# A two-layer attention kernel: the bias table made before the first projection, products of ones in two pauses of the array, and layer 1's weights prepared in the first image

## The chip, the cores and the metric

The kernel runs on one core of a Trainium2 chip. A core has a matrix engine (TensorE, PE in the profile), a vector engine (VectorE, DVE), an engine for activation functions (ScalarE, ACT), a general engine (GpSimd, POOL) and a sequencer that mostly issues transfers (SyncE, SP). Each runs its own list of instructions in order and waits for the others by semaphores. Sixteen DMA engines move data between the memory (DRAM) and the on-chip buffers; SP and ACT put transfers on queues for them. The metric is the device time of one execution in microseconds (us), lower is better.

## The reference, cut to what matters

Eight images of 384 channels and 32 x 32 = 1024 positions pass through two layers in float32. Layer 0 normalizes by groups and applies attention with a position bias, the output of a small network on the relative offset of two positions:

```python
def relative_bias(h, w, w1, b1, w2, b2):
    rel = (coords[:, None, :] - coords[None, :, :]) / denom      # 2 numbers per pair
    hidden = gelu(rel @ w1 + b1)                                 # 192 wide
    return transpose(hidden @ w2 + b2, (2, 0, 1))                # 8 heads

# layer 0 (8 heads of 48)
q, k, v = split(group_norm(x) @ qkv_w + qkv_b)
attn = softmax(q @ k.T * 48**-0.5 + relative_bias(...))
x = x + (attn @ v) @ proj_w + proj_b

# layer 1 (6 heads of 64), on tokens t
q, k, v = split(layer_norm(t) @ qkv_w.T)
q, k = normalize(q), normalize(k)        # each row: less its mean, over its deviation
t = t + (softmax(q @ k.T * 64**-0.5) @ v) @ proj_w.T + proj_b
t = t + bitlinear(gelu(bitlinear(layer_norm(t))))
```

The bias depends only on the offset, so 63 x 63 values per head hold all of it. Layer 1's projection comes after a layer normalization and, for q and k, before a normalization of each head's row. Both means can be taken out of the weights ahead of time: each column of the transposed weight less its mean over the 384 input channels, and each head's 64 columns of q and k less their mean.

## The kernel before, in words

**Layer 0's work.** `_layer0` (line 184) runs the eight images one after another. For each image, `project_qk` (456) makes q and k: three pairs of heads, each with a `pq` tile of 128x1024 for q and one for k, twelve matmul records per tile. Tiles for q are evicted from PSUM by DVE, those for k by ACT. `project_v` (490) makes four `pv` tiles, evicted by DVE. Then 32 units follow: a unit is a pair of heads, a half of the queries and a quarter of the keys. `scores` (514) writes two `s` tiles in PSUM, DVE adds the bias (`e<-s,grow`, line 532), ACT takes the exponential (536), and two units later `weigh` (542) multiplies by v into `o`. All the PSUM tiles come from one pool of four (`mm2`, 111): a fifth tile waits until the first is evicted.

**The bias.** `hidden` (342) runs the network's first layer on the offsets (`rel`, `w1`): 32 matmul records into eight `ph` tiles, and eight Gelu activations on ACT. `table_part` (366) multiplies by `w2` into `pb`, DVE adds `b2`, and SP stores the part to `table` in DRAM, half of the table per call. The attention needs the bias spread out, as `grow` in the on-chip buffer, in 32 parts (8 heads, 4 blocks of rows). `grow_load` (384) fetches a part from `table` with four DMAs of 114.2 KB (`wide<-table`), and `grow_turn` (396) copies it, reversed, into `grow`: even blocks on ACT (401), odd ones on DVE (403). Twenty parts go through a pool of nine `e` tiles, twelve through rows of `oT`, which is where attention outputs go later.

**The order of work.** The engines' lists are in the order in which the Python code calls them. `_Later` (64) delays work: `after(n, work)` has `work` called at the n-th following `step()`. There is a step after each of the six `pq` tiles, each of the four `pv` tiles and each unit. Before the change the start is: group norm's statistics, the weights placed (`place_weights_qk`, 289), both calls of `hidden`, the loads of `bqk`, the normalization applied on DVE, the loads of `wv`, `bv`, `wp`, `wl`, `bp` (`load_weights_v_out`, 318), the first `table_part`, and the second one a step later. Loads of parts begin at step 2, turns one step after their loads.

**Transfers.** All these loads but those of the bias network are issued by SP, in order. Each DMA of SP and ACT reports on one of eight semaphores, taken in turn in program order, and an issue waits until the former transfer on its semaphore has landed.

**Layer 1's weights.** `_Start` (121) loads layer 1's weight (1.77 MB) during the last image of layer 0, at its unit 5, and layer 1's first image at unit 6. Then `means` makes the column sums by products with a tile of ones (`cm`, line 146: twelve records of 128x512 and six of 128x128), ACT scales them (151), POOL subtracts them (158); `heads` sums each head's columns on DVE (164) and subtracts on POOL (166). These steps are called at units 10 to 23.

Of the kernel before, what the change touches and what calls it, by code (L numbers as in the profile page):

```python
# [63 lines left out]
class _Later:  # L64


    def __init__(self):
        self.due = []
# [52 lines left out]
class _Start:  # L121
# [4 lines left out]
    def __init__(self, tc, ins, x1, shared):  # L126
        self.nc, self.ins, self.x1, self.shared = tc.nc, ins, x1, shared

    def load_weights(self):
        self.wqkv = self.shared.weights("wqkv").rearrange("p (k c) -> p k c", k=KC)  # L130
        self.nc.sync.dma_start(
            self.wqkv, self.ins["L1_attn_qkv_wT"].rearrange("(k p) c -> p k c", p=P)
        )
# [5 lines left out]
    def means(self, temp, at, n):  # L139
        nc = self.nc  # L140
        pm = self.shared.mm2(f"cm{at}")
        for h in range(-(-n // HALF)):
            w = min(HALF, n - h * HALF)
            for k in range(KC):
                cols = slice(at + h * HALF, at + h * HALF + w)
                nc.tensor.matmul(
                    pm[:, h, :w], self.shared.ones, self.wqkv[:, k, cols],
                    start=(k == 0), stop=(k == KC - 1),
                )
        self.mean = temp(f"cmean{at}")  # L150
        nc.scalar.activation(
            self.mean[:, :n], pm.rearrange("p h q -> p (h q)")[:, :n], AF.Copy, scale=1.0 / C
        )

    def subtract(self, at, n):
        for k in range(KC):
            w = self.wqkv[:, k, at : at + n]
            self.nc.gpsimd.tensor_sub(w, w, self.mean[:, :n])

    def heads(self, k):  # L160
        nc = self.nc
        w = self.wqkv[:, k, 0 : 2 * C].rearrange("p (h d) -> p h d", d=D1)
        hm = self.shared.pool.tile([P, 2 * H1], F32, tag="hm", name=f"hm{k}")
        nc.vector.tensor_reduce(hm, w, AX.X, ALU.add)
        nc.gpsimd.tensor_scalar(hm, hm, 1.0 / D1, 1.0, ALU.mult, ALU.mult)
        nc.gpsimd.tensor_sub(w, w, hm.unsqueeze(2).to_broadcast([P, 2 * H1, D1]))

    def stages(self, temp):

        first, rest = (0, 2 * HALF), (2 * HALF, 3 * C - 2 * HALF)  # L170
        return [
            (5, self.load_weights),
            (6, self.load_image),
            (10, lambda: self.means(temp, *first)),
            (11, lambda: self.subtract(*first)),
            (12, lambda: self.means(temp, *rest)),
            (14, lambda: self.subtract(*rest)),
            (19, lambda: self.heads(0)),
            (21, lambda: self.heads(1)),
            (23, lambda: self.heads(2)),  # L180
        ]


def _layer0(tc, ins, x1, sums, shared, beside):
# [9 lines left out]
    with ExitStack() as ctx:  # L194
# [31 lines left out]
        QT, QN = 32, 2 * HALF  # L226
# [5 lines left out]
        nc.vector.memset(rel, 0.0)  # L232
        nc.vector.memset(w2, 0.0)
        nc.vector.memset(b2, 0.0)
        for g in range(P // QT):
            at = g * QN
            n = min(QN, NREL - at)
            nc.scalar.dma_start(rel[g * QT : g * QT + 2, 0:n], ins["rel"][:, at : at + n])
            nc.scalar.dma_start(w1[g * QT : g * QT + 2], ins["L0_conv_mlp_w1"])
        with nc.allow_non_contiguous_dma(reason="a bias, once"):  # L240
            nc.scalar.dma_start(b1, ins["L0_conv_mlp_b1"].rearrange("(k p) -> p k", p=HC))
            nc.scalar.dma_start(
                w2[:, :, 0:H0], ins["L0_conv_mlp_w2"].rearrange("(k p) h -> p k h", p=HC)
            )
        for g in range(P // QT):
            nc.scalar.dma_start(b2[g * QT : g * QT + H0], ins["L0_conv_mlp_b2"].unsqueeze(1))
# [9 lines left out]

# [31 lines left out]

        def place_weights_qk():
            whole = 2 * NF0 * D0  # L290
            for s in range(2):
                nc.vector.tensor_copy(
                    wqk[:, :, s, :, 0:D0],
                    raw[:, :, s, 0:whole].rearrange("p k (h d) -> p k h d", d=D0),
                )
                for j in range(2):
                    at = whole + j * D0
                    nc.vector.tensor_copy(
                        wqk[:, :, s, j::2, D0:S0],
                        raw[:, :, s, at : at + D0].rearrange("p k (c d) -> p k c d", d=FR),  # L300
                    )

        def load_bias_qk():
            with nc.allow_non_contiguous_dma(reason="a bias, once"):
                for j in range(2):
                    for row, n, at, step in (
                        (j * S0, D0, j * D0, 2 * D0),
                        (j * S0 + D0, FR, (2 * NF0 + j) * D0, FR),
                    ):
                        for s in range(2):  # L310
                            nc.sync.dma_start(
                                bqk[row : row + n, s],
                                bass.AP(
                                    qkv_b.tensor, qkv_b.offset + s * C + at, [[1, n], [step, NF0]]
                                ),
                            )

        def load_weights_v_out():
            nc.sync.dma_start(wv, qkv_w[:, 2 * C : 3 * C].rearrange("(k p) c -> p k c", p=P))
            nc.sync.dma_start(bv, qkv_b[2 * C : 3 * C].partition_broadcast(P))  # L320
            pw = ins["L0_conv_proj_w"]
            for j in range(2):
                last = (2 * NF0 + j) * D0
                for row, n, at, step in (
                    (j * S0 + SP, D0, j * D0, 2 * D0),
                    (j * S0, FR, last, FR),
                ):
                    nc.sync.dma_start(
                        wp[row : row + n],
                        bass.AP(  # L330
                            pw.tensor, pw.offset + at * C, [[C, n], [step * C, NF0], [1, C]]
                        ),
                    )
                nc.sync.dma_start(wl[j * S0 + SP : (j + 1) * S0], pw[last : last + D0])
            with nc.allow_non_contiguous_dma(reason="a bias, once"):
                nc.sync.dma_start(bp, ins["L0_conv_proj_b"].rearrange("(k p) -> p k", p=P))
# [3 lines left out]
        WR = GW // 4  # L340

        def hidden(r):

            hids = {}
            for k in range(2):
                for a in range(2):
                    ph = mm2(f"ph{r}{k}{a}")
                    for i in range(2):
                        g = 2 * a + i
                        nc.tensor.matmul(  # L350
                            ph[0:HC, i], w1[g * QT : g * QT + 2, ts(k, HC)],
                            rel[g * QT : g * QT + 2, ts(r, HALF)], start=True, stop=True,
                        )
# [12 lines left out]
        def table_part(r, hids):  # L366
            pb = mm2(f"pb{r}")
            for k in range(2):
# [6 lines left out]
            nc.vector.tensor_scalar_add(backwards(part[:, HALF - 1 : HALF], HALF), pb[:, 0], b2)  # L375
            for g in range(P // QT):
                at = g * QN + r * HALF
                n = min(HALF, NREL - at)
# [264 lines left out]
        place_weights_qk()  # L643
        hids = [hidden(r) for r in range(2)]
        stages[3]()
        load_bias_qk()
        stages[4](nc.vector)
        load_weights_v_out()
        table_part(0, hids[0])
        later.after(1, lambda: table_part(1, hids[1]))  # L650
        nc.scalar.activation(tiny[:, 1:2], tiny[:, 0:1], AF.Exp)
# [14 lines left out]
        for i, n in enumerate((3, 3, 3, 3, 2, 2, 2, 2)):  # L666
            later.after(i + 3 + (i > 3), lambda n=n: grow_turns(n))
            later.after(i + 2, lambda n=n: grow_loads(n))
        for i in range(len(parts) - 20):
            later.after(i + 11, lambda: grow_turns(1))  # L670
            later.after(i + 8, lambda i=i: grow_loads(1, 1 + i % NF0))
        qk = project_qk(0, first)
        project_v(0, first)
        with_last = beside(etile)
        for b in range(B):
            held = []
            for i, u in enumerate(units):
# [10 lines left out]
                if b == B - 1:  # L688
                    for at, work in with_last:
# [1130 lines left out]
def tile_conv_attn_hybrid(ctx: ExitStack, tc: tile.TileContext, ins, out):  # L1820
    dram = ctx.enter_context(tc.tile_pool(name="x1", bufs=1, space=DRAM))
    x1 = dram.tile([B, C, N], F32, tag="x1", name="x1")
    state = ctx.enter_context(tc.tile_pool(name="state", bufs=1))
    flag = state.tile([P, 1], mybir.dt.int32, tag="flag", name="flag")
    sums = state.tile([P, B, NP0, 2 * N // P], F32, tag="sums", name="sums")
    with ExitStack() as main, tc.manual_schedule():
        shared = _Shared(tc, main)
        start = _Start(tc, ins, x1, shared)
        before = _layer0(tc, ins, x1, sums, shared, start.stages)
# [6 lines left out]
    with tc.If(out_of_range > 0):  # L1836
        _layer0_shifted(tc, ins, x1)
        with ExitStack() as again, tc.manual_schedule():
            shared = _Shared(tc, again)
            start = _Start(tc, ins, x1, shared)  # L1840
            late = again.enter_context(tc.tile_pool(name="late", bufs=2))
            for _, stage in start.stages(
                lambda name: late.tile([P, N], F32, tag="t", name=name)
            ):
                stage()
# [45 lines left out]
```

## Time and profile before

| what | value |
|---|---|
| median of 3 runs | 3036.66 us (3036.26 to 3038.47) |
| profiled execution's own time | 3039.49 us |
| its span, first to last instruction | 3037.7 us, mean granted clock 0.998 |
| PE busy | 3017.8 us, 99% of the span |
| DVE, ACT, POOL busy | 1775.4, 1401.8, 464.2 us |
| chain that ended last | PE 93%, DMA 3%, DVE 2%, ACT 1% |
| first hidden matmul | 7.41 us |
| first `pq` matmul / first `s` matmul | 23.14 / 73.87 us |

The table comes from the page of the profile and its timeline. All times inside the execution count from the span's start. "Busy" is the time in which an engine carries out instructions, without issuing transfers or waiting. The timeline puts neighbouring instructions of one kind on one row: start, duration, engine, line, operation, tile written and tiles read, and their number; in brackets how long the engine was idle before and what ended it. "PE" are matmuls, "PEld" the loads of their weights, "SPq" and "ACTq" the issue of transfers. One 128x512 float32 product is two matmul records. The granted clock is the share of TensorE's full clock, 1.00 or half of it.

### The profile page before, as it was taken

The page shows a single profiled execution, that of the slowest core. Times are in us where ns is not written, and L with a number is a line of the kernel's source. Part 1 is how long each engine was busy: PE and PEld are TensorE (multiplying, and loading weights), DVE is VectorE, ACT ScalarE, POOL GpSimd, SP SyncE. Part 2 cuts the span into 40 slices and gives each one's busy share as a digit, 9 for nine tenths or more (in the row PEclk, how much of TensorE's full clock was granted, in tenths as well). Part 3 has the DMA queues.
Part 4 walks back from the last instruction along what each step waited for, and adds up shares of the span by engine and source line. Part 5 has one row for each costly group of instructions (what it writes and reads, how often), then busy time and mean ns, then how long its engine had stood idle before and what let it go on. Part 6 is the DMA issues. An engine that isn't in the chain of part 4 may idle for free.

```text
span 3037.7 us, 45667 instructions
## 1 busy us (share of the span) xinstructions
PE 3017.8 (99%) x18914; PEld 1616.1 (53%) x18914; DVE 1775.4 (58%) x1763; ACT 1401.8 (46%) x1759; POOL 464.2 (15%) x315
## 2 busy tenths in 40 slices
PE   9999999999999999999999999999999999999999
PEld 3455546455554645444545655655655655645453
DVE  3746647373654727355564765765765755754646
ACT  2633526253442616244373563553553553553534
POOL 0111102121110202123202202202202202211110
PEclk9999999999999999999999999999999999999999
DMA  7412021211202020121311101101101101102011
GB/s 175 122 26 83 19 82 23 65 37 23 78 21 81 23 78 23 29 96 51 99 43 31 56 16 37 50 16 37 50 23 30 50 23 30 50 16 72 16 51 38
DMA packets 102137, 149.94 MB, mean 49 GB/s; under 512 B 59616, under 2 KB 63184, under 8 KB 101152
## 3 DMA queue, kind: packets, MB, share of 16 engines
q1 hardware_dynamic: 99056, 146.86, 17.2%
q8 instruction: 152, 2.49, 0.3%
q14 instruction: 65, 0.53, 0.1%
q10 hardware_dynamic: 2864, 0.05, 0.1%
HBM read 110.52 MB, written 27.30 MB: 45 GB/s over the span
## 4 chain that ended last, share of the span: by engine, by line
PE 93%; DMA 3%; DVE 2%; ACT 1%; POOL 0%; issue 0%; SPq 0%; DVEq 0%; ACTq 0%; POOLq 0%
PE s L521 15%; PE o L552 15%; PE s L1322 11%; PE o L1371 11%; PE pq L467 8%; PE y2p L1614 6%; PE pq L1178 5%; PE pp L616 4%; PE pv L1259 4%; PE y1p L1563 4%; PE pp L1468 4%; PE pv L495 4%; PE sum L1398 1%; DMA wide<-table 1%; PE hs L1207 1%; DVE lun L1515 1%
## 5 line engine op out<-in xcount | busy, mean ns | idle before, releaser
L536 ACT ACTIVATE e<-e 128x1024 f32<-128x1024 f32 x512 | 535.0, 1057 | 441.7 <-DVE e L532 421.7
L532 DVE TENSOR_TENSOR e<-s,grow 128x1024 f32<-128x1024 f32 x512 | 601.0, 1217 | 190.6 <-PE s L521 190.1
L521 PE MATMUL s<-qk 48*64 48x512 f32 x4096 | 608.0, 592 | 2.6 <-DVE e L532 2.2
L552 PE MATMUL o<-e,v 64*64 64x512 f32 x4096 | 603.5, 591 | 0.0
L1333 ACT ACTIVATE e<-s,kc 128x512 f32<-128x512 f32 x768 | 463.3, 693 | 171.7 <-PE s L1322 161.0
L1322 PE MATMUL s<-qk,qk 64*64 64x512 f32 x3072 | 418.5, 592 | 0.3
L1371 PE MATMUL o<-e,v 64*64 64x512 f32 x3072 | 414.9, 590 | 0.0
L521 PEld LDWEIGHTS s<-qk 48*64 48x64 f32 x4096 | 238.8, 133 | 227.5 <-issue 82.9
L552 PEld LDWEIGHTS o<-e,v 64*64 64x64 f32 x4096 | 259.8, 133 | 178.6 <-issue 76.8
L1348 DVE TENSOR_TENSOR t<-t,e 128x1024 f32<-128x1024 f32 x192 | 230.8, 1221 | 54.0 <-ACT e L1333 53.9
L1322 PEld LDWEIGHTS s<-qk,qk 64*64 64x64 f32 x3072 | 153.8, 132 | 190.0 <-issue 108.8
L1178 PE MATMUL pq<-bx,wqkv 128*128 128x512 f32 x576 | 254.1, 596 | 0.7 <-ACT tra L1150 0.7
L467 PE MATMUL pq<-xn,w 128*128 128x512 f32 x576 | 251.7, 598 | 0.0
L1371 PEld LDWEIGHTS o<-e,v 64*64 64x64 f32 x3072 | 158.2, 133 | 170.5 <-issue 142.9
L581 POOL TENSOR_TENSOR inv<-sums,over 128x16 f32<-128x16 f32 x32 | 92.7, 2898 | 1011.0 <-DMA sums<-sd 852.6
L467 PEld LDWEIGHTS pq<-xn,w 128*128 128x128 f32 x576 | 109.6, 191 | 142.9 <-issue 140.4
L1178 PEld LDWEIGHTS pq<-bx,wqkv 128*128 128x128 f32 x576 | 107.9, 190 | 143.4 <-issue 139.7
L1345 DVE TENSOR_TENSOR t<-e,e 128x1024 f32<-128x1024 f32 x96 | 114.1, 1223 | 81.2 <-ACT e L1333 81.0
L1550 DVE TENSOR_REDUCE parts<-y 128x1 f32<-128x1024 f32 x75 | 90.0, 1217 | 93.1 <-ACT y L1547 92.5
L1228 POOL TENSOR_TENSOR hc<-hc,rsqrt 128x32 f32<-128x32 f32 x24 | 139.4, 5810 | 2.0
L1194 ACT ACTIVATE qsq<-pq 128x1024 f32<-128x1024 f32 x48 | 49.1, 1024 | 190.3 <-DVE qk L1188 102.0
L477 DVE TENSOR_SCALAR qk<-pq,bqk 128x1024 f32<-128x1024 f32 x24 | 30.8, 1284 | 176.9 <-PE pq L467 176.9
(165 smaller groups left out, 3033.9 us busy)
## 6 DMA issues: line engine op xcount, KB each, us to landing
rb<-rd SPq DMA_DIRECT2D x110, 256.0 KB
xn<-in_x_dram SPq DMA_DIRECT2D x24, 512.0 KB
res<-in_x_dram SPq DMA_DIRECT2D x24, 512.0 KB
x<-res SPq DMA_DIRECT2D x24, 512.0 KB
bx<-x SPq DMA_DIRECT2D x8, 1536.0 KB
rq<-hi SPq DMA_DIRECT2D x48, 256.0 KB
out_dram<-bx SPq DMA_DIRECT2D x23, 512.0 KB
wide<-table SPq DMA_DIRECT2D x80, 114.2 KB
```

The source lines that it names most:

```text
L467: nc.tensor.matmul(pq[:, h], wqk[:, k, s, 2 * pair : 2 * pair + 2, :].rearrange("p h d -> p (h d)"), xn[:, k, ts(h, HALF)], start=(k == 0) ...
L521: nc.tensor.matmul(s[j][ts(c, QP), i], qk[pair][rows, 1, ts(4 * m2 + 2 * i + c, QP)], qk[pair][rows, 0, ts(h, HALF)], start=True, stop=True,)
L532: nc.vector.tensor_add(e.rearrange("p (i q) -> p i q", i=2), s[j], bass.AP(near.tensor, near.offset, [near.ap[0], [-QROWS * IW, 2], [1, HA ...
L536: nc.scalar.activation(e, e, AF.Exp)
L552: nc.tensor.matmul(po[ts(j, S0), r], v[keys, 2 * m2 + i, 2 * pair + j, :], es[j][keys, ts(i, HALF)], start=(m2 == 0 and i == 0), stop=(m2 ...
L1178: nc.tensor.matmul(pq[:, h], wqkv[:, k, s * C + pair * P : s * C + (pair + 1) * P], xt[:, k, ts(h, HALF)], start=(k == 0), stop=(k == KC - 1),
L1228: nc.gpsimd.tensor_tensor(c, c, rsqrt.to_broadcast(list(c.shape)), ALU.pow)
L1322: nc.tensor.matmul(s[j][ts(c, QP), i], qk[pair, 1][rows, ts(4 * m2 + 2 * i + c, QP)], qk[pair, 0][rows, ts(h, HALF)], start=True, stop=True,)
L1333: nc.scalar.activation(e[:, ts(i, HALF)], s[j][:, i], AF.Exp, scale=kc[:, pair, j, m : m + 1])
L1348: nc.vector.tensor_add(total[j], total[j], e)
L1371: nc.tensor.matmul(po[ts(j, D1), r], v[keys, 2 * m2 + i, at : at + D1], es[j][keys, ts(i, HALF)], start=(m2 == 0 and i == 0), stop=(m2 == ...
L1614: nc.tensor.matmul(py[m][:, h], w2[:, k, ts(m, P)], supply.parts[k][i][:, ts(h, HALF)], start=(k == 0 and i == 0), stop=(k == FC - 1 and i ...
```

## The change

- **Operands of the network.** `rel` is cut evenly and loaded with two DMAs instead of four, `w1` likewise; only one column is cleared. ACT calls a Gelu on a small tile early and loads `w2` and `b2` after it.
- **Products of ones.** `stir` multiplies the tile of ones by itself, n times, into a PSUM tile that the next real product overwrites: seven before the first hidden product, four before the first table half.
- **Table.** Both halves are made before the first projection, the first evicted by DVE and the second by ACT.
- **Loads moved.** `bqk`, `wv`, `bv`, `wp`, `wl` and `bp` are issued by ACT instead of SP.
- **Layer 1's weights.** `_Weights` loads them in the first image by ACT, ahead of `wv`, into rows of `grow` that are filled last. Column sums are now made by two additions of the three row blocks on POOL and three products; DVE scales, POOL subtracts, `heads` as before; SP stores the result to `ready` in DRAM. In the last image of layer 0 only a load of `ready` and the load of the image are left.
- **Spreading the table.** The first three parts are loaded before `project_qk`, the others two steps earlier than before, and the turns a step earlier; for the last twelve parts loads and turns come two steps later.

```diff
+    def load(self, here, mean):
+        self.w = here.rearrange("p (k c) -> p k c", k=KC)
+        self.mean = mean
+        self.nc.scalar.dma_start(
+            self.w, self.ins["L1_attn_qkv_wT"].rearrange("(k p) c -> p k c", p=P)
         )
+    def add(self):
+        for k in range(1, KC):
+            self.nc.gpsimd.tensor_add(self.mean, self.w[:, 0] if k == 1 else self.mean, self.w[:, k])
+
+    def means(self):
+        self.sums = []
+        for at in range(0, 3 * C, 2 * HALF):
+            pm = self.shared.mm2(f"cm{at}")
...
+                self.nc.tensor.matmul(
+                    pm[:, h, :w], self.shared.ones, self.mean[:, cols], start=True, stop=True
+                )
+            self.sums.append((at, n, pm.rearrange("p h q -> p (h q)")))
+
+    def take(self):
+        for at, n, pm in self.sums:
+            self.nc.vector.tensor_scalar_mul(self.mean[:, at : at + n], pm[:, :n], 1.0 / C)
+
+    def subtract(self, k):
+        self.nc.gpsimd.tensor_sub(self.w[:, k], self.w[:, k], self.mean)
...
-            (10, lambda: self.means(temp, *first)),
-            (11, lambda: self.subtract(*first)),
-            (12, lambda: self.means(temp, *rest)),
-            (14, lambda: self.subtract(*rest)),
-            (19, lambda: self.heads(0)),
-            (21, lambda: self.heads(1)),
-            (23, lambda: self.heads(2)),
...
+    def store(self):
+        self.nc.sync.dma_start(self.ready, self.w.rearrange("p k c -> p (k c)"))
...
+        late = grow[:, H0 - 3 :].rearrange("p h w x -> p (h w x)")
+        early = late[:, GW * IW : GW * IW + KC * 3 * C], late[:, 0 : 3 * C]
...
-            nc.sync.dma_start(wv, qkv_w[:, 2 * C : 3 * C].rearrange("(k p) c -> p k c", p=P))
-            nc.sync.dma_start(bv, qkv_b[2 * C : 3 * C].partition_broadcast(P))
+            nc.scalar.dma_start(wv, qkv_w[:, 2 * C : 3 * C].rearrange("(k p) c -> p k c", p=P))
+            nc.scalar.dma_start(bv, qkv_b[2 * C : 3 * C].partition_broadcast(P))
...
+        def stir(bank, n):
+
+            for _ in range(n):
+                nc.tensor.matmul(
+                    bank.rearrange("p (a b) -> p a b", b=P), shared.ones,
+                    shared.ones.unsqueeze(1).to_broadcast([P, HALF // P, P]), start=True, stop=True,
+                )
...
         place_weights_qk()
+        nc.scalar.activation(tiny[:, 1:2], tiny[:, 0:1], AF.Gelu)
+        load_hidden_rest()
         hids = [hidden(r) for r in range(2)]
         stages[3]()
+        for r in range(2):
+            table_part(r, hids[r])
         load_bias_qk()
+        nc.scalar.activation(tiny[:, 1:2], tiny[:, 0:1], AF.Exp)
+        weights.load(*early)
+        load_weights_v_out()
         stages[4](nc.vector)
-        load_weights_v_out()
-        table_part(0, hids[0])
-        later.after(1, lambda: table_part(1, hids[1]))
-        nc.scalar.activation(tiny[:, 1:2], tiny[:, 0:1], AF.Exp)
+        for at, work in (
+            (2, weights.add), (4, weights.means), (5, weights.take), *(
+                (at + k, lambda k=k, work=work: work(k))
+                for at, work in ((5, weights.subtract), (7, weights.heads)) for k in range(KC)
+            ), (10, weights.store),
+        ):
+            later.after(at, work)
...
         for i, n in enumerate((3, 3, 3, 3, 2, 2, 2, 2)):
-            later.after(i + 3 + (i > 3), lambda n=n: grow_turns(n))
-            later.after(i + 2, lambda n=n: grow_loads(n))
-        for i in range(len(parts) - 20):
-            later.after(i + 11, lambda: grow_turns(1))
-            later.after(i + 8, lambda i=i: grow_loads(1, 1 + i % NF0))
+            later.after(i + 2 + (i > 3), lambda n=n: grow_turns(n))
+            if i == 0:
+                grow_loads(n)
+            else:
+                later.after(i, lambda n=n: grow_loads(n))
+        for i in range(4 * H0 - 20):
+            later.after(i + 13, lambda: grow_turns(1))
+            later.after(i + 10, lambda i=i: grow_loads(1, 1 + i % NF0))
```

## The prediction

> **What bounds the kernel now.** I read the page first, then the PE waits of the start, the timeline and the table of windows of the first image, and last the PE timeline of the last layer-0 image, where the removed work sits.
>
> ```profile
> PE 3017.8 (99%) x18914; PEld 1616.1 (53%) x18914; DVE 1775.4 (58%) x1763; ACT 1401.8 (46%) x1759; POOL 464.2 (15%) x315
> ...
> PE ph L350 <- DMA w<-in_L_conv_mlp_w_dram: 7.4, 1, 7.4
> PE s L521 <- DVE e L532: 2.2, 1, 2.2
> PE s L521 <- DVE v L500: 0.4, 1, 0.4
> ```
>
> PE is busy for 99% of the span, so time is gained only where PE stands, runs at half clock, or gets fewer instructions. It stands 7.4 us for its first operands and 2.6 us around the first scores. The timeline of the start (columns: start, duration, work, idle before and its releaser):
>
> ```profile
> 7.41 12.24 PE L350 MATMUL ph<-rel,w 2*96 2x512 f32 x32 [7.41 <-DMA w<-in_L_conv_mlp_w_dram]
> 12.16 1.28 ACT L355 ACT_TABLE_LOAD   x1 [12.16 <-DMA b<-in_L_conv_mlp_b_dram]
> 13.46 8.12 ACT L355 ACTIVATE hid<-ph,b 96x1024 f32<-96x1024 f32 x8
> 23.14 7.52 PE L467 MATMUL pq<-xn,w 128*128 128x512 f32 x12
> 30.59 1.92 PE L370 MATMUL pb<-hid,w 96*32 96x512 f32 x16
> 35.04 1.23 SPq L391 DMA_DIRECT2D wide<-table  x3
> ```
>
> The first projection begins at 23.14, with matmuls 0.853 us apart until 27.40 and 0.429 after it. The second half of the table is squeezed in at 30.59, and only at 35.04 can SP begin the loads that spread the table. Then the first scores:
>
> ```profile
> 58.30 15.64 PE L495 MATMUL pv<-w,xn 128*128 128x384 f32 x48
> 79.97 2.34 DVE L532 TENSOR_TENSOR e<-s,grow 128x1024 f32<-128x1024 f32 x2
> 81.24 4.82 PE L521 MATMUL s<-qk 48*64 48x512 f32 x16 [2.20 <-DVE e L532]
> 83.86 0.65 DVE L403 COPY grow<-wide 128x480 f32<-128x480 f32 x1 [1.55 <-DMA wide<-table]
> 85.61 0.60 ACT L401 COPY grow<-wide 128x480 f32<-128x480 f32 x1 [1.73 <-DMA wide<-table]
> 89.04 1.45 PE L521 MATMUL s<-qk 48*64 48x512 f32 x9
> ```
>
> Scores begin at 73.87; the fourth unit's begin at 89.04, 15.2 us later, where the later images take 7.4 (1.77 + 1.72 + 3.88). So 7.8 us are lost, and the releaser is the stream of table parts: DVE's and ACT's turn copies, in order before the `e` adds, wait for loads. PE's idleness in this stretch is followed by half clock (82.0 to 88.8). The stream is held by the DMA engines (columns of busy time by engine, granted clock, DMA share, GB/s):
>
> ```profile
> 32.50:58.30 25.80, 25.80 (x63) 11.46 (x61) 5.83 (x7) 4.94 (x7) 0.00 (x0) 1.00 0.89 191
> 58.30:73.90 15.60, 15.60 (x53) 8.96 (x51) 4.74 (x9) 3.10 (x5) 0.00 (x0) 1.00 1.05 220
> 73.90:89.00 15.10, 12.46 (x65) 3.42 (x65) 8.95 (x11) 5.69 (x7) 0.00 (x0) 0.77 0.94 235
> ```
>
> From 35.04 to the landing at 85.1, 21 parts of four loads go through: 50.1 / 84 = 0.596 us a load, against 0.42 us to issue one. At the other end, PE's timeline in the last image of layer 0:
>
> ```profile
> 1336.23 2.15 PE L552 MATMUL o<-e,v 64*64 64x512 f32 x16
> 1338.31 5.42 PE L146 MATMUL cm<-wqkv,ones 128*128 128x512 f32 x12
> 1343.65 1.95 PE L521 MATMUL s<-qk 48*64 48x512 f32 x16
> ...
> 1350.69 0.94 PE L146 MATMUL cm<-wqkv,ones 128*128 128x128 f32 x6
> ```
>
> Neighbours are 1.72 apart. The first step takes 7.42, the second 2.69 (1348.86 to 1351.55): 5.70 + 0.97 = 6.67 us.
>
> **What the Trainium skill says.** "DMA: Bandwidth & Descriptors", section "Issuing engines are not separate DMA queues": transfers of SP and ACT run on the same 16 engines and interleave; a second issuing engine saves only issue time. The 0.94 to 1.05 shares above say that the engines, not issue alone, are the limit here. "TensorE: Matmul & The Clock Gate", Part 1: the array runs at half rate until it has been busy for a while, and an idle stretch returns it to half rate; the trace agrees, 0.853 against 0.429 us a record, and half clock after the idle before 81.24. "ScalarE: Activation LUTs", section "What ACT_TABLE_LOAD costs": a table load is an instruction on ACT; the trace has 1.28 us.
>
> **The change part by part.**
>
> *Start.* `rel` and `w1` come in four DMAs for eight, the Gelu table is loaded before the operands are there, `w2` and `b2` after it: ACT could begin the gelus some 4 us earlier (12.16 + 1.28 against about 8). But PE first runs seven products of ones: 14 records x 0.853 = 11.9 us cold, or about 6.8 cold and 2.6 warm, 9.4, from about 1.0. The hidden products follow at 10.4 to 12.9, the first gelu about 1.3 later, and eight take 8.12: end 20 to 22, against 21.58. Nothing to lose here, about 1 to gain. Four more products (3.4 warm, 6.8 cold) run beside the last gelus; two table halves at 1.92 warm or 3.64 cold follow. So pq begins at about 24 to 28; I take 25.5.
>
> *Projection.* Before, pq takes 23.14 to 58.30 = 35.2: 72 x 0.429 = 30.9, 1.95 for the table half and some 2.1 of cold clock. After: 30.9 plus the column sums of layer 1's weights (four products 128x512 and two 128x128 records each: 4 x 0.429 + 2 x 0.11 = 1.94). 25.5 + 32.8 = 58.3: PE's own path does not move. All that can be gained in the first image is the 7.8 us at the first scores, and only if the stream is early enough.
>
> *The stream.* Table halves ready at about 23 and 26, eight stores on SP (7.84 from 26.90 before, with a wait of 3.4 for the second half; some 4 without) and the stream starts at about 31.2, 3.8 earlier. With 80 loads at 0.596 it would land at 31.2 + 47.7 = 78.9. Added to the same engines in this stretch: layer 1's weights, 1.77 MB, at the 400 GB/s that the first loads reach (398 and 409 in the DMA row) = 4.4 us; and `wv`, `bv`, `wp`, `wl`, `bp`, 1.5 MB, which before ran ahead of the stream: a share of 0.76 over 23.1 to 32.5 = 7.1. The idle share of before takes some: 0.11 x 25.8 + 0.06 x 11 = 3.5. Extra 4.4 + 7.1 - 3.5 = 8.0, so the twentieth part lands at about 86.9. Bounds: 5.5, if more of the slack is used, and 15, below.
>
> *First scores.* All 20 turns now stand ahead of the first `e` add (before, 18 did, and the add ran at 79.97). After the last landing: turn 0.65, two adds 2.35, then the third unit's scores and the first `o`, 3.44 warm or 6.88 at half clock, since PE stands meanwhile. The fourth unit's scores: 86.9 + 6.4 to 9.9 = 93.3 to 96.8, middle 95.0, against 89.04: **+6.0**.
>
> *ACT.* Nine loads that SP issued now stand on ACT, with the eight of `bqk`. Program order gives each DMA one of eight completion semaphores in turn, and an issue waits for the former user: `wl` waits for `wv`, the second `wp` for `bv`, and so on, so ACT is held until nearly all have moved: 4.4 + 7.1 = 11.5 us after the weights' issue (about 31), half as much again with the stream beside them: to 43 to 49. Queued behind: the eviction of the second pq tile, whose PSUM slot PE needs at 25.5 + 4 x 5.15 = 46, then three turns and the fourth tile's eviction. PE stalls 2.6 to 9.5 us. It is free as long as the stream is later still: unstalled, the `e` adds would be reached at about 75, so 10 to 12 us of stall are covered. Without that cover it costs its full length.
>
> *Weights in the first image.* Adds and subtractions on POOL (128x1024 in 2.37; five of 1152 columns, 13.4), three head reductions on DVE (0.94), subtractions on POOL (1.47): POOL is idle there, DVE's 2.8 + 1.5 lie beside waits for the stream. The store `ready` (1.77 MB, 4.4 us of engines) stands in SP's order ahead of the last 12 parts, which have three units (10.3) between load and turn. Between 0 and 4.4; I take **1.8**.
>
> *Layer 0's end.* The sums, **-6.7**; subtractions and heads on other engines were hidden anyway. The 1.77 MB load remains.
>
> Sum: 6.0 + 1.8 - 6.7 = +1.1, on a span of 3037.7; the profiled run's own 3039.49 lies 1.8 above its span and 2.8 above the median 3036.66. Against the median: about 3038.
>
> **Rivals.**
> (a) *The stream is not late*: smaller loads only fill gaps of issue. If it lands at 78.9 to 81 and the clock stays full, the fourth scores begin at 85 to 87: -2 to -4, and with -6.7, -9 to -11: 3026 to 3028. With the whole 7.8 won it would be -14, 3022. For it: issue takes 0.42 us, under the 0.596. Against: shares of 0.94 and 1.05.
> (b) *SP stands behind ACT's transfers* (slower): a semaphore is shared by the weights' load and the seventh table load, and by `wp`, `wl` and the loads of later parts. If the two rings get half the engines each, the weights land some 9 us after issue instead of 5, the chain behind them takes its 18, and SP stands at its seventh, fifteenth and later loads: extra 15 for 8. Last part at 94, scores at 100.3 to 103.8, +13; + 1.8 - 6.7 = +8: 3045; up to 3048 with the store's 4.4. It decides from an extra of about 13.
> (c) *The change doesn't warm the clock*: pq starts cold at 25.5 to 28 and PE's path is 2 to 5 later; hidden by the stream, unless (a) holds, where the gain shrinks to -5.
>
> **How the numbers follow.** This kernel's measurement tells 0.2%, 6.1 us, from no change. The forecast (+1, from -5 to +6) gets 0.45; (a) 0.20; (b) and a stalled PE beyond its cover 0.30; (c) 0.05. Some of the forecast's upper edge lies over +6. So faster 0.20, within 0.42, slower 0.38. The range: 3029 (part of (a) in) to 3048 (b's upper end); the forecast's own is 3032 to 3043.
>
> **What would show it.** In the changed profile: pq at 24 to 28 and full clock; the first `wide` load at about 31; the weights' transfer beside it; the last turn of the twenty at 85 to 89, with its wait for `wide`; ACT's first eviction not before 43; the fourth scores at 93 to 97; no `cm` at 1338. I am wrong if the stream lands before 82 or after 93, or if PE's stall in pq exceeds 12 us.

## The result and the profile after

The changed kernel takes 3047.23 us in the median of seven runs (3043.30 to 3049.25), the kernel before beside it 3037.58 (3036.01 to 3038.47): ratio 1.003, 95% interval 1.002 to 1.004. It is slower by some 9.7 us. The profiled executions differ by 9.3 in span (3047.0 against 3037.7).

To see where, I compared the start of each exponential of ACT in the two traces, one by one; all 1280 are there in both. The offset is the start in the changed kernel less the start in the kernel before, in us: fourth unit of the first image +9.85; 29th unit +15.30; the last image of layer 0, once layer 1's weights would have been prepared, +8.31; end of layer 1's attention +9.30. So there is a loss of 9.85 at the start, another of 5.45 later in the first image, a gain of 6.99 at layer 0's end, and 0.99 that drifts in along layer 1, where the program is the same.

PE's waits in the changed kernel (what waited for what, total us, times, longest), the largest five in the first 400 us, one of them left out:

```profile
PE pq L501 <- ACT qk L515: 7.0, 1, 7.0
PE s L555 <- DVE e L566: 4.5, 2, 2.4
...
PE cm L148 <- ACT qk L515: 0.8, 1, 0.8
PE cm L148 <- POOL grow L138: 0.4, 1, 0.4
```

PE now stands 8.2 us in the projection, mostly for an eviction by ACT. The timeline of the changed kernel tells why:

```profile
25.80 20.84 PE L501 MATMUL pq<-xn,w 128*128 128x512 f32 x48
...
30.89 0.44 ACTq L132 DMA_DIRECT2D grow<-in_L_attn_qkv_wT_dram  x1
...
48.65 1.11 ACT L515 ACTIVATE qk<-pq,bqk 128x1024 f32<-128x1024 f32 x1 [16.34 <-DMA wp<-in_L_conv_proj_w_dram]
...
57.28 12.38 PE L501 MATMUL pq<-xn,w 128*128 128x512 f32 x24 [6.97 <-ACT qk L515]
...
90.02 0.65 DVE L437 COPY grow<-wide 128x480 f32<-128x480 f32 x1 [2.65 <-DMA wide<-table]
90.59 4.61 DVE L566 TENSOR_TENSOR e<-s,grow 128x1024 f32<-128x1024 f32 x4
...
98.63 0.59 PE L555 MATMUL s<-qk 48*64 48x512 f32 x1
```

The weights' load is issued at 30.89 and, by its semaphore, has landed at 41.6, 10.7 us later. ACT stands in its own issues until 48.65. PE waits until 57.28 and comes back at half clock. The last of the twenty turns runs at 90.02 (the last two before: 83.86 on DVE and 85.61 on ACT), and the fourth unit's scores begin at 98.63 instead of 89.04. The first four adds then run in one go (4.61 us): their scores had been ready and they waited for the turn, which stands ahead of them on DVE. So these 9.6 us have two parts. DVE's last turn is 6.2 later. From that turn to the fourth unit's scores it takes 8.6 instead of 5.2, which is 3.4 more: with the turns a step earlier, the first unit's two adds (2.3 us) stand behind the last turn as well, where before they ran at 79.97, ahead of it. SP's waits in the same kernel, 20 to 90 us:

```profile
SPq L425 <- DMA grow<-in_L_attn_qkv_wT_dram: 8.0, 1, 8.0
...
SPq L425 <- DMA wp<-in_L_conv_proj_w_dram: 1.5, 1, 1.5
```

The table of windows of the changed kernel (busy us by engine, then clock, DMA share, GB/s):

```profile
10.00:21.00 11.00, 10.66 (x38) 3.73 (x39) 2.85 (x7) 8.12 (x8) 1.25 (x4) 0.69 0.06 7
...
32.00:58.00 26.00, 17.83 (x42) 7.63 (x41) 3.28 (x5) 4.09 (x7) 5.21 (x2) 0.93 1.00 249
58.00:74.00 16.00, 16.00 (x38) 7.53 (x37) 5.39 (x8) 3.49 (x5) 6.69 (x3) 0.91 1.00 233
```

The DMA engines do next to nothing from 10 to 21 us (share 0.06) and are full from 32 to 74 (1.00). The second loss lies at units 14 to 18, again by the timeline:

```profile
133.99 3.62 SPq L425 DMA_DIRECT2D oT<-table  x8
...
138.09 0.59 ACT L435 COPY grow<-oT 128x480 f32<-128x480 f32 x1 [2.51 <-DMA oT<-table]
...
143.15 2.83 PE L555 MATMUL s<-qk 48*64 48x512 f32 x11 [2.13 <-DVE e L566]
```

The last two parts are issued only at 133.99, in SP's order behind the transfers of the first division, whose last wait is for POOL. Their turns come late, the exponentials and adds behind the turns come late, PE stands 2.13 us, and the records of half clock run from 142.9 to 149.7.

In the last image of layer 0 PE's scores and outputs follow each other 1.72 apart with no `cm` between them, as the change intended.

### The profile page after: what moved, and what is told of

It reads as the page before. It is cut to its first block, busy times and chain, and to the rows that moved or that the text cites. A ratio compares the mean times of both kernels' runs of the same rounds, so it can differ in the third digit from the quotient of the medians.

```text
span 3047.0 us, 45684 instructions
## 1 busy us (share of the span) xinstructions
PE 3022.9 (99%) x18924; PEld 1606.7 (53%) x18924; DVE 1775.8 (58%) x1764; ACT 1401.6 (46%) x1759; POOL 470.1 (15%) x314
## 4 chain that ended last, share of the span: by engine, by line
PE 90%; DVE 2%; DMA 2%; POOL 0%; ACT 0%; issue 0%; SPq 0%; DVEq 0%; ACTq 0%; POOLq 0%
PE s L555 14%; PE o L586 14%; PE s L1368 11%; PE o L1417 11%; PE pq L501 7%; PE y2p L1660 6%; PE pq L1224 5%; PE pp L650 4%; PE pv L1305 4%; PE y1p L1609 4%; PE pp L1514 4%; PE pv L529 4%; PE sum L1444 1%; PE hs L1253 1%; DVE lun L1561 1%; DVE un L1556 1%
## 5 line engine op out<-in xcount | busy, mean ns | idle before, releaser
L586 PEld LDWEIGHTS o<-e,v 64*64 64x64 f32 x4096 | 253.1, 134 | 186.5 <-issue 89.9
L1417 PEld LDWEIGHTS o<-e,v 64*64 64x64 f32 x3072 | 158.4, 133 | 170.3 <-issue 142.8
L1305 PE MATMUL pv<-wqkv,bx 128*128 128x384 f32 x384 | 131.9, 497 | 0.0
```

What stands on the lines that cost most here:

```text
L586: nc.tensor.matmul(po[ts(j, S0), r], v[keys, 2 * m2 + i, 2 * pair + j, :], es[j][keys, ts(i, HALF)], start=(m2 == 0 and i == 0), stop=(m2 ...
L1305: nc.tensor.matmul(pv[:, i, 0:C], xt[:, k].rearrange("c (p m) -> c m p", m=MT)[:, 2 * m2 + i], wqkv[:, k, 2 * C : 3 * C], start=(k == 0), ...
L1417: nc.tensor.matmul(po[ts(j, D1), r], v[keys, 2 * m2 + i, at : at + D1], es[j][keys, ts(i, HALF)], start=(m2 == 0 and i == 0), stop=(m2 == ...
```

## The experiments

Theory A: ACT, held in its own issues, keeps PE waiting, and that delay sets the first scores. Theory B: the table parts arrive late because of the bytes beside them and SP's stand behind the weights; PE's stall is covered. All diffs are against the changed kernel unless said otherwise. The table shows each run's median, its ratio to the kernel before on the same chip, and offsets of exponentials against the trace of before (fourth unit; 29th unit; after the weights' place in the last image of layer 0). An offset comes from one execution of each kernel. By their spans these differ from the medians: the idle window's trace lies 9.6 us under the trace of before, its median 6.2 under the median. In five kernels whose program is the same up to the first projection (the change, bulk on SP, out weights later, last parts earlier, and out later with old steps) pq begins between 25.8 and 27.1. So a difference of offsets of 1 or 2 us between runs says nothing by itself.

| run | median us | ratio, 95% interval | 4th | 29th | weights |
|---|---|---|---|---|---|
| the change | 3047.23 | 1.0030 (1.002 to 1.004) | +9.85 | +15.30 | +8.31 |
| bulk on SP | 3045.33 | 1.0028 (1.0017 to 1.0040) | +8.58 | +11.04 | +4.09 |
| out weights later | 3041.94 | 1.0016 (1.0009 to 1.0023) | +3.79 | +6.44 | -0.52 |
| no early weights | 3051.47 | 1.0046 (1.0029 to 1.0063) | +5.71 | +8.81 | +8.58 |
| last parts earlier | 3044.79 | 1.0024 (1.0015 to 1.0033) | +11.03 | +11.03 | +4.08 |
| no products of ones | 3043.79 | 1.0020 (1.0011 to 1.0028) | +5.89 | +11.53 | +4.54 |
| out later, old steps | 3037.17 | 0.9995 (0.9987 to 1.0004) | +4.09 | +3.73 | -3.24 |
| idle window | 3032.13 | 0.9979 (0.9971 to 0.9986) | -3.43 | -3.67 | -10.66 |
| weights at end | 3040.62 | 1.0007 (0.9998 to 1.0016) | -2.19 | -2.19 | +2.09 |
| idle window, no ones | 3032.35 | 0.9981 (0.9973 to 0.9989) | -2.40 | -2.40 | -9.39 |
| idle window, second ones | 3031.90 | 0.9980 (0.9972 to 0.9989) | +0.90 | +0.66 | -6.31 |
| weights' load alone | 3040.20 | 1.0010 (1.0001 to 1.0018) | +3.73 | +8.57 | +1.58 |

**Bulk loads on SP.**

```diff
-            nc.scalar.dma_start(wv, qkv_w[:, 2 * C : 3 * C].rearrange("(k p) c -> p k c", p=P))
+            nc.sync.dma_start(wv, qkv_w[:, 2 * C : 3 * C].rearrange("(k p) c -> p k c", p=P))
...
```

> The changed kernel with wv, bv, wp, wl and bp issued by SP again, at the same place of the program (after the table's stores, ahead of the first part); all bytes stay. Theory A (ACT, held by its own issues, keeps PE waiting for the eviction of pq, and that delay sets the first scores): PE's wait of 7.0 us for ACT's eviction falls under 1, scores begin near 76 instead of 85, the fourth unit's near 91 instead of 99, total 3038 to 3040. Theory B (the stream of table parts is late by its bytes and by SP's stand behind the weights, and PE's stall is covered by it): PE's wait falls as well and scores begin near 76, but the twentieth part still lands at 88 to 92 and the fourth unit's scores begin at 96 to 100; total 3045 to 3049.

PE's wait did not go away:

```profile
PE pq L501 <- ACT qk L515: 7.1, 1, 7.1
```

ACT no longer stands in its own issues, but its next eviction is queued behind turns, and SP, busy with the bulk, issues its first part only at 42.9. Both theories missed the wait; the fourth unit moves by 1.3, the last turn is at 89.78. So moving the issues from one engine to the other moves the place of the wait and not the time.

**The output weights after the parts.**

```diff
+        def load_weights_out():
             pw = ins["L0_conv_proj_w"]
...
-                    nc.scalar.dma_start(
+                    nc.sync.dma_start(
                         wp[row : row + n],
...
         load_weights_v_out()
+        later.after(30, load_weights_out)
```

> The changed kernel with wp, wl and bp (0.73 MB, first needed in the second image) issued by SP at step 30, after the parts. ACT has then only wv and bv behind the weights. A: ACT is released near 41 instead of 48.6, its eviction no longer holds PE (wait 0 to 2 for 7.0), fourth scores 5 to 8 us earlier, total 3039 to 3042. B: 0.73 MB less in the stretch bring the twentieth part 2 to 3 us earlier, and the total falls by 2 to 3, to about 3045.

PE's wait fell to 3.5 and the last turn from 90.02 to 84.99: 0.73 MB fewer in the stretch, and shorter waits of ACT and SP, bring 6.1 at the fourth unit. The run cannot say which theory is right, since both delays fell together.

**No early weights.** The class of the kernel before is put back, with its steps in the last image.

```diff
-        weights.load(*early)
         load_weights_v_out()
...
-            (2, weights.add), (4, weights.means), (5, weights.take), *(
...
```

> The changed kernel without its weights part: layer 1's weights are loaded and prepared at layer 0's end as in the kernel before, the rest of the change stays. A: ACT is released 8 to 10 us earlier, no wait of PE in pq, first scores at 75 to 77. B: SP no longer stands 8.0 us at its seventh table load and 1.77 MB less run beside the stream: the twentieth part at 80 to 82 instead of 90.0, fourth scores at 88 to 91 instead of 98.6. Layer 0's end costs its 6.7 again. Both give 3043 to 3046 with the loss of 5.4 near unit 14 still there, 3038 to 3040 if that comes from the store of the weights.

This run shows that A is not the whole cause. PE never waits in the projection, and its scores begin at 73.46 (before: 73.87). Yet:

```profile
73.46 1.95 PE L551 MATMUL s<-qk 48*64 48x512 f32 x16
...
85.95 0.65 DVE L433 COPY grow<-wide 128x480 f32<-128x480 f32 x1 [4.09 <-DMA wide<-table]
86.52 4.61 DVE L562 TENSOR_TENSOR e<-s,grow 128x1024 f32<-128x1024 f32 x4
87.79 3.96 PE L551 MATMUL s<-qk 48*64 48x512 f32 x13 [2.10 <-DVE e L562]
...
94.49 0.59 PE L551 MATMUL s<-qk 48*64 48x512 f32 x1
```

The first add waits until 86.52 for the last of the twenty turns (85.95), 6.6 later than before (79.97). A is not enough: with PE free in the projection, the fourth unit still loses 5.7 (5.5 by its scores). But late parts are not all of this: DVE's last turn is only 2.1 later than before (83.86), and ACT's last one earlier than before (83.86 for 85.61). The other 3.4 lie between the turn and the scores (8.5 for 5.2): the order of the turns. PE also waits 4.7 us there for evictions of v that stand behind turns on DVE. Starting the stream 3.3 us earlier (31.7 for 35.0) brought almost nothing, its last issue is at 81.4 for 82.4, though one part fewer goes through it by then: what ran ahead of it before, `wv` to `bp`, now runs beside it. I had expected 80 to 82 for the last part; it was 85.9. The loss near unit 14 was still there (3.1), so the store of the weights is not needed for it. The total, 3051.47, lies over the 3043 to 3046 that I had put down.

**The last twelve parts two steps earlier.**

```diff
-            later.after(i + 13, lambda: grow_turns(1))
-            later.after(i + 10, lambda i=i: grow_loads(1, 1 + i % NF0))
+            later.after(i + 11, lambda: grow_turns(1))
+            later.after(i + 8, lambda i=i: grow_loads(1, 1 + i % NF0))
```

> The changed kernel with loads and turns of the last twelve parts two steps earlier, at 8 and 11 as in the kernel before. If the 5.4 us lost at units 13 to 16 come from the later steps (the last two loads queue on SP behind the division's transfers, ACT's turn waits for them, and PE's idleness brings half clock), the loss goes: total 3041 to 3043. If they come from the store of the weights on SP, the loss stays and the total is 3046 to 3048.

The offset stays at 11.03 from the fourth unit to the 29th: the whole second loss comes from the later steps. In all six kernels with the later steps the loss between these units is 2.5 to 5.6, in the other six, which have the steps of before, it is gone (0.0 to -0.4). The total fell by 2.4 in the median, to 3044.79, less than 5.45 and outside the 3041 to 3043; in this trace the last turn was 0.8 later and the fourth unit 1.2.

**No products of ones.**

```diff
-                    if not (r or k or a):
-                        stir(ph[:, 0], 7)
...
-            if r == 0:
-                stir(pb[:, 1], 4)
```

> The changed kernel without the products of ones. If the first image is set by the stream of table parts and ACT's held issues, the products are worth nothing here: pq starts within 2 us of 25.8 but cold for some us, PE's wait for ACT's eviction shrinks by what pq is slower, the fourth unit's scores and the total stay within 2 us (3045 to 3049). If a warm array at pq is what counts, the total rises by 2 to 5, to 3049 to 3052.

pq began at 22.70 instead of 25.80, the stream moved with it (first part at 28.0 for 30.7, last turn 87.09 for 90.02), and the fourth unit came 4 us earlier. In the median the difference is 3.4, with intervals that overlap. I had the stream's start down as independent of the products; it isn't, as the table is made behind them.

**Output weights later, and the turns and the last parts at the steps of before.** Against the second run:

```diff
-            later.after(i + 2 + (i > 3), lambda n=n: grow_turns(n))
+            later.after(i + 3 + (i > 3), lambda n=n: grow_turns(n))
...
-            later.after(i + 13, lambda: grow_turns(1))
-            later.after(i + 10, lambda i=i: grow_loads(1, 1 + i % NF0))
+            later.after(i + 11, lambda: grow_turns(1))
+            later.after(i + 8, lambda i=i: grow_loads(1, 1 + i % NF0))
```

> wp, wl and bp after the parts as in the run before, and in addition the turns of the first twenty parts a step later and loads and turns of the last twelve two steps earlier, both as in the kernel before; layer 1's weights still in the first image behind the table. If the last turns ahead of the first adds, and the last twelve parts behind the division, each cost what the offsets of the traces say (about 3 and 2.7 us), the total is 3035 to 3038. If the first adds are set by the landing of the parts alone whatever the order, only the 2.7 come off: 3039 to 3040.

3037.17, no different from the kernel before, and 4.8 under the second run. The loss near unit 14 is gone. The first add ran at 81.44 for 85.56, but the fourth unit gained nothing (+4.09 for +3.79): its adds stand behind the later turns, and DVE's last turn was itself 1.4 later (86.39 for 84.99). From that turn to the fourth unit's scores it took 5.1 for 7.3, so the order of before is worth some 2 us here. PE's wait in the projection went as well, which fits that turns ahead of the evictions on ACT were part of it.

**Loads in the idle window.** Against the run just told, one block of issues moves:

```diff
         load_hidden_rest()
+        weights.load(*early)
+        load_weights_v_out()
         hids = [hidden(r) for r in range(2)]
...
-        weights.load(*early)
-        load_weights_v_out()
```

> The same, with layer 1's weights, wv and bv issued by ACT right after b2, at about 9 us, where the DMA engines of the changed kernel are idle for some ten us. If bytes beside the stream are the cause of the loss, they are then gone from it: no wait of PE for ACT's eviction, SP doesn't stand at its seventh table load, the twentieth part lands at 75 to 80, the fourth unit's scores begin at 81 to 85, and with 6.7 less at layer 0's end the total is 3023 to 3029. If the stream is limited by its own 80 loads (0.6 us each however little runs beside it), the twentieth part lands at 81 to 83, and the total is 3030 to 3034.

3032.13, ratio 0.9979: faster than both kernels. The windows of this run, the same stretches as above:

```profile
10.00:21.00 11.00, 9.30 (x36) 3.27 (x29) 2.85 (x7) 8.12 (x8) 0.28 (x2) 0.60 0.72 266
...
32.00:58.00 26.00, 26.00 (x63) 11.62 (x62) 6.21 (x7) 6.36 (x9) 0.00 (x0) 1.00 0.86 226
```

The bytes have moved from the full stretch to the idle one. The first add is early, and PE goes from units to outputs without a stop:

```profile
76.65 6.41 PE L557 MATMUL s<-qk 48*64 48x512 f32 x48
...
78.71 2.35 DVE L568 TENSOR_TENSOR e<-s,grow 128x1024 f32<-128x1024 f32 x2 [0.37 <-issue]
...
82.90 1.95 PE L588 MATMUL o<-e,v 64*64 64x512 f32 x16
```

The fourth unit gains 7.5 on the run before it, and its scores begin at 84.64, within the 81 to 85 of the first alternative; the total lies above its 3023 to 3029, in the range of the second. From the first to the last of the 80 loads of parts it is now 43.3 us (32.3 to 75.6), in the run before it 51.0 (31.6 to 82.6): the stream was held by what ran beside it. In this run PE's path sets the first scores.

**Layer 1's weights at the end, with additions ahead of the sums.** Against the run with the idle window:

```diff
-        weights.load(*early)
...
+    def add(self, temp, at, n):
+        self.mean = temp(f"cmean{at}")[:, :n]
+        for k in range(1, KC):
+            w = [self.wqkv[:, i, at : at + n] for i in (0, k)]
+            self.nc.gpsimd.tensor_add(self.mean, w[0] if k == 1 else self.mean, w[1])
...
+            (9, lambda: self.add(temp, *first)),
+            (11, lambda: self.means(*first)),
```

> As the run with loads in the idle window, but layer 1's weights are loaded and prepared in the last image, as before, with POOL adding the three row blocks ahead of the column sums, so that PE does 1.94 us of sums for 6.36. Against that run: first image 0 to 2 us earlier (no sums, no store of 1.77 MB beside the last parts), layer 0's end about 2 to 4 us dearer; total 3025 to 3032. If early weights cost the first image more than they spare, it is the faster of the two.

3040.62, a miss: the first image was 1.2 to 1.5 later, not earlier, and my placing of the sums cost a new wait, seen in PE's waits between 1300 and 1400 us:

```profile
PE cm L149 <- POOL cmean L143: 5.5, 1, 5.5
```

POOL was in a division when the additions were due, PE stood, and 6.8 us of half clock followed. The run says nothing on well placed sums.

**The idle window without products of ones, and with the second group alone.**

```diff
-                    if not (r or k or a):
-                        stir(ph[:, 0], 7)
...
-            if r == 0:
-                stir(pb[:, 1], 4)
```

> The run with the loads in the idle window, without the products of ones. There PE's own path sets the first scores (pq begins at 28.2 and PE never waits from there to the units), so now its start counts: without products pq begins at 23 to 25, some 2 us of it cold, the fourth unit's scores come 2 to 4 us earlier, total 3028 to 3030. If the warm clock is worth its delay, the total stays at 3032 or rises to 3034.

> The same with only the four products ahead of the first table half. They run while ACT finishes its gelus; if they delay the table half (they took 5.9 us with the seven before them), pq begins 1 to 3 us later than without any and the total lies 1 to 3 above it; if they fill a pause and warm the array, pq begins at the same time and warm, and the total lies up to 2 below it.

3032.35 and 3031.90: no difference from 3032.13 that these runs can tell. With the second group alone pq began at 29.33, with a full clock, and the fourth unit was 3.3 later than without any; the median doesn't show it. Without products pq began at 27.74, hardly before the 28.16 with all of them, and for another reason:

```profile
25.14 3.89 DVE L480 TENSOR_SCALAR xn<-xn,gsc 128x1024 f32<-128x1024 f32 x3 [2.12 <-DMA gsc<-back]
...
27.74 2.69 PE L499 MATMUL pq<-xn,w 128*128 128x512 f32 x3 [2.60 <-DVE xn L480]
```

Group norm's small transfers come later with the early loads: the statistics go out at 8.46 and are fetched back only at 17.55, in the changed kernel at 8.87 and 11.84. Then the three multiplications of the image take 3.89 us instead of 2.25, while POOL adds the weights' blocks beside them. My 23 to 25 for pq left both out.

**The weights' load alone.** The smallest edit of the change itself: one line earlier, all else as changed.

```diff
         load_hidden_rest()
+        weights.load(*early)
         hids = [hidden(r) for r in range(2)]
...
-        weights.load(*early)
         load_weights_v_out()
```

> The changed kernel with a single line moved: layer 1's weights are issued by ACT right after b2 instead of after the table; wv, bv, wp, wl, bp stay on ACT behind the table, all steps stay. If the 1.77 MB beside the stream are the main cause, SP no longer stands at its seventh load, ACT's first eviction comes near 42 for 48.6, PE waits 0 to 2 for it, the last of the twenty turns comes near 86 for 90.0 (as in the run without early weights), the fourth unit's offset falls from 9.9 to about 5 and the total to 3040 to 3043. If ACT's other nine loads hold it as long, PE's wait stays over 4 and the total over 3044.

3040.20 for 3047.23. ACT's first eviction came at 42.07, PE's wait fell from 7.0 to 2.9, the last turn came at 84.43 for 90.02, and the fourth unit's offset fell by 6.1, from 9.85 to 3.73:

```profile
84.43 0.65 DVE L437 COPY grow<-wide 128x480 f32<-128x480 f32 x1 [3.56 <-DMA wide<-table]
...
92.51 0.59 PE L555 MATMUL s<-qk 48*64 48x512 f32 x1
```

The place of this one transfer is worth 6 to 7 us (6.6 with each kernel held against the kernel before beside it), some two thirds of what the change lost. PE's wait was a little over the 0 to 2 that I had put down. Of the 3.5 that the fourth unit's scores still lose, 0.6 is the last turn (83.86 before) and 2.9 come after it (8.1 for 5.2), the order of the turns again.

The stream's length in all the runs, from the first to the last of its 80 loads, goes with the bytes of ACT's loads beside it: 43.0 to 44.4 us in the four runs that have none, 49.7 and 50.9 with 1.5 MB (no early weights; weights' load alone), 51.0 and 51.5 with 2.6 MB (the two runs with output weights later and the weights behind the table), 56.2 to 56.6 with all 3.3 MB (the change, last parts earlier, no products). With the bulk on SP most bytes go ahead of the stream; it then takes 44.0 but starts 12 later, and ends where the change's does. No run separates the bytes from SP's stand of 8.0 at its seventh load, but the DMA share during that stand, from 33.6 to 41.6, is 1.02: the engines were full without the stream.

## Why the prediction was right or wrong

The time lies in the range, at its upper end; the value given as likeliest, 3038, was 9 too low, and a slower kernel had been given 0.38. What happened lies between the forecast and rival (b): SP did stand behind the weights' load, as (b) has it, but the last turn (90.0) and the fourth unit's scores (98.6) fall between the forecast's 86.9 and 95.0 and (b)'s 94 and 100.3. That the total comes out beside (b)'s 3045 is in part luck: the first loss is smaller than (b)'s 13, and the second is larger than the 1.8, with a cause that no term had.

*Start: right.* pq began at 25.80 (25.5 taken), the parts' loads at 30.66 (31.2), ACT's first eviction at 48.65 (43 to 49), PE's stall was 8.2 (2.6 to 9.5). That there was "nothing to lose" before the table was wrong: the run without products started pq 3.1 and the parts 2.6 earlier.

*The stream: mechanism right, size off.* The sum put 4.4 us for the weights and 8.0 of extra in all, with the last part at 86.9. The weights took 10.7 from issue to landing beside the parts (7.1 when issued at 9.15, in the run that moves their load alone). SP stood 8.0 at its seventh load, and the last turn was at 90.0: with the stream's start at 30.7, so a base of 30.7 + 47.7 = 78.4, an extra of 11.6, where (b) was to decide from about 13. In the run without early weights it is 85.9 - (31.7 + 47.7) = 6.5, where 7.1 - 3.5 = 3.6 would follow from the prediction: so the 3.5 of idle engine time that I let absorb bytes seem hardly to have been there. The other 5.1 is the weights, with SP's stand in it, for the 4.4 put down.

*First scores: right.* From the last turn at 90.02 to the fourth unit's scores at 98.63 it is 8.6, within 6.4 to 9.9. That all twenty turns would stand ahead of the first add was in the sum.

*PE's stall covered: right here, but the two are not apart.* Scores began at 85.07 and the adds at 90.59, so the 8.2 of stall did not set the end. But the turns stand ahead of evictions on ACT, so the stream also lengthens the stall; the two are one chain and not two paths.

*Last parts: mis-sized.* Between 0 and 4.4, 1.8 taken; measured 5.45. The term had priced the store of the weights; the cause is the two steps by which loads and turns moved, which put two parts behind the first division on SP. PE's stand itself is 2.13; the 6.8 us of half clock after it add the rest.

*Layer 0's end: right.* -6.7 predicted, -6.99 measured, and -6.95 to -6.99 in the nine other runs that prepare them in the first image.

*Left out:* 0.99 along layer 1, which is the same program. Along layer 1 the offset changed by -0.8 to +2.8 in the other runs, upwards in all but one, always against the one trace of before. It is taken for variation between executions; nothing here shows that.

With the measured terms, 9.85 + 5.45 - 6.99 + 0.99 = 9.30, the difference of the spans.

## What to carry to other kernels

Look at the DMA engines' share by stage before choosing the place of a transfer: the same 1.77 MB cost 6 to 7 us more in a full stretch than in an idle one 20 us earlier. An issue list on a computing engine that waits for shared completion semaphores blocks that engine's evictions, and a moved step has to be followed into the order of every queue that it enters: here the last parts behind the division, and the first adds behind the last turn. When a stretch is set by a stream of transfers, an earlier start of the stream is worth little if the transfers that ran ahead of it then run beside it.

## What the runs showed of the hardware that was not expected

The full clock that follows the seven products was lost again while PE was busy by the profile (the ends of its matmuls are modelled). In the changed kernel the clock was full from 6.35 to 13.18 and half until 20.00, though PE's busy time in the table of windows of that kernel was 3.04 of 3.38 us and then 6.82 of 6.82:

```profile
9.80:13.18 3.38, 3.04 (x23) 0.88 (x22) 2.06 (x6) 2.18 (x3) 0.00 (x0) 1.00 0.18 33
13.18:20.00 6.82, 6.82 (x18) 2.51 (x17) 0.79 (x1) 5.94 (x6) 1.25 (x4) 0.50 0.04 1
```

What ran at the point of loss were hidden products, with two rows of operands. The Trainium skill ("TensorE: Matmul & The Clock Gate", Part 1) speaks of idle windows; here the profile shows a busy one at the point of loss. In all nine kernels with the first products the same loss is seen, 6.8 us after the full clock was granted; no run isolates its cause, and the 0.34 us in which PE waited at 11.82 is not excluded. With the second group alone, ahead of the table half, the clock was full from 24.2 on without a loss until the end.
